# Reads ahead of rank passes, a table step inside the first product, and a reordered head and tail in a graph kernel

## The chip, the cores and the metric

The kernel runs on one core of a Trainium2 chip. The metric is the time of one execution on the device in microseconds (us); several runs are made and their median is taken. A profile of one further execution gives every instruction's start and duration, and the TensorE clock that was granted.

## The reference

x holds 32 graphs of 512 channels by 1024 nodes, f32. Layer 0 is an attention whose score for a pair of nodes is a leaky relu of a sum of two numbers, one of each node; layer 1 multiplies by the elementwise square of the adjacency, with its mask. Each layer is followed by a residual addition and a layer norm over the nodes.

```python
def _L0_gnn_ref(x, wq, wk, wm, bm):
    q = jnp.einsum('c,bcn->bn', wq, x)
    k = jnp.einsum('c,bcn->bn', wk, x)
    scores = q[:, None, :] + k[:, :, None]
    scores = jnp.where(scores > 0, scores, NEG_SLOPE * scores)
    att = jax.nn.softmax(scores, axis=-1)
    agg = jnp.einsum('bcn,bmn->bcm', x, att)
    out = jnp.einsum('oc,bcm->bom', wm, agg) + bm[None, :, None]
    return jax.nn.relu(out)

def _L1_gnn_ref(x, support, kernel, bias):
...
    W = support * kernel
    out = jnp.einsum('bnf,nm->bmf', x, W)
    out = out + bias
    return out

x = _layernorm(x + _L0_gnn_ref(x, L0_gnn_wq, L0_gnn_wk, adj, L0_gnn_bm), axis=-1)
x = _layernorm(x + _L1_gnn_ref(x, adj, adj, L1_gnn_bias), axis=-1)
```

## The kernel before

**Layer 0 without the matrix of scores.** A score depends on the sum of q of one node and k of another, so each side of the leaky relu is a product of an exponential of q and one of k. The nodes are sorted by q. Then, for every node, the nodes with a positive score are one end of the sorted list and the rest the other, and a softmax-weighted sum is a combination of two prefix sums, looked up at the place where k cuts the list. The steps for one graph:

- `project`: for each of 8 groups of 128 nodes, TensorE multiplies x by the weights with wq and wk beside them (8 matmuls of 128x257 into a PSUM tile `zp`); ScalarE copies it to `zrow`. Column 0 is q, the last column k.
- `peak`: VectorE takes the maximum of q and sets k aside. `spread` spreads q over the partitions (TensorE transposes `qb`, `mx`).
- `place`: the rank passes. For each of 8 node groups VectorE compares 128x1024 numbers and sums up (`lt`, 1.28 us), and a small instruction makes the index `ranki` of each pair of groups. `send` (GpSimd) writes the rows of `zrow` to DRAM (`td`) in sorted order with an indirect DMA. `count` (ScalarE) finds where k cuts the list. `fetch` (SyncE's DMA queue) brings the sorted rows back in 9 blocks, `zs`.
- `weigh`: ScalarE makes the exponentials `w`, VectorE the triangular matrices `lq`; part 0 for the first table step, part 1 for the others. `table`: 9 steps (0 to 8) of running sums. Each has 8 matmuls into `tp`, a ScalarE copy to `ts`, one row of which GpSimd (L425) and one ScalarE copy into the blocks of the next step; SyncE stores `ts` to `td`. So each step waits for the row copies of the one before.
- `share` makes the indices, `pick` (GpSimd) gathers the rows with 8 indirect DMAs into `rows`. `own`, `norm`, `scale` and `gain` weigh and add the parts of a row (`shares` is `own` and `norm`). `turn` transposes and adds the bias with a relu, `join` adds the residual x and takes layer-norm statistics; `root`, `shift` and `apply` finish the norm, `y`.

**Layer 1** is a product with the 512x512 matrix w1 (adj squared elementwise, plus identity), written as 7 products of quarters, as in Strassen's method: A11, S1, S2, S3, A22, S4, A12. Each has two halves, `mul[2n]` and `mul[2n+1]` (m = 0, 1) of two accumulation steps. Their operands are `sums` T1 to T4 of quarters of y, which VectorE makes, and their results are combined by VectorE `reads`: c1 reads A11, c5 S1, u2 S2, u3 S3, "21" A22, "12" S4, "11" A12, while u4 and "22" only add what was read before.

**Tiles.** PSUM has three large tiles in the pool `ps_mm` and one in `ps_t`. A new tile waits until one is released by its last reader. So A22 needs the tile that c5 reads, S4 the one of u2.

**Order.** All is issued in an order written out by hand, and each engine (TensorE, VectorE, ScalarE, GpSimd, and the DMA queues of SyncE and ScalarE) works its own instructions off in that order. Three graphs are in work at a time. `begin` projects graphs 0 to 2 and sorts and tabulates graph 0; `opening` finishes graph 0 up to its norm. `slot(s)`, 29 times, projects graph s + 2 (`new`), tabulates s + 1 (`mid`), finishes layer 0 of s and normalises and stores s − 1 (`old`). It ends with `phase`: the product of s, with picks of `mid` and rank passes and sends of `new` in between. `end` finishes the last two graphs with `rest` (a product with a hook `after(i)` behind each half) and `last`.

In `phase` the order for VectorE is: ranks 0 and 1, T2, c1 first half, ranks 2 and 3, T3, c1 second half, T4, ranks 4 and 5, c5, ranks 6 and 7, u2, u3, u4, 22, 21, then `shares` of picks 0 to 3, 12, two gains, 11, two gains. For GpSimd it is picks 0, 1, sends 0, 1, picks 2, 3, sends 2, 3, pick 4, pick 5, sends 4, 5, pick 6, sends 6, 7, pick 7. The ninth table step of `mid` stands ahead of `phase`, behind `spread`.

In the preamble, ScalarE's queue loads wq, wk, bm (as 4-byte pieces, one for each partition) and the bias of layer 1; SyncE's queue loads adj, then x. VectorE has copies of the transposed weights (L196), wq and wk (L197, L198), the squaring (L202) and a subtraction of the bias (L209) in this order of the program; the page's lines below show when each ran. In the middle of `begin`'s third loop all 8 picks of graph 0 are issued, and a copy of one element (L807) stands ahead of `fetch(1)`: it reads a picked row and writes into `zs`, so that the larger part of the fetch starts behind the fourth pick.

Of the kernel before, what the change touches and what calls it, by code (L numbers as in the profile page):

```python
# [23 lines left out]
def gat_gcn_resnorm_kernel(  # L24
# [46 lines left out]
    nc = tc.nc  # L71
# [36 lines left out]
    wq_sb = const.tile([P, CT], F32, name="wq_sb")  # L108
    nc.scalar.dma_start(out=wq_sb, in_=wq.rearrange("(t p) -> p t", p=P))
    wk_sb = const.tile([P, CT], F32, name="wk_sb")  # L110
    nc.scalar.dma_start(out=wk_sb, in_=wk.rearrange("(t p) -> p t", p=P))
    bm_sb = const.tile([P, CT], F32, name="bm_sb")
    nc.scalar.dma_start(out=bm_sb, in_=bm.rearrange("(t p) -> p t", p=P))
    bias_bc = const.tile([P, N], F32, name="bias_bc")
    nc.scalar.dma_start(out=bias_bc, in_=bias.partition_broadcast(P))
# [50 lines left out]
    for b in range(3):  # L166
        for ct in range(CT):
            load(b, ct)

# [17 lines left out]
    for ct in range(CT):  # L187
        pt = ps_mm.tile([P, C], F32, name=f"pt_{ct}", tag="mm")
        for ot in range(CT):
            nc.tensor.transpose(  # L190
                pt[:, ot * P : (ot + 1) * P], adj_sb[:, ot, ct * P : (ct + 1) * P], ident
            )
        if ct % 2:
            nc.scalar.copy(wmT[:, ct, 1 : C + 1], pt)
        else:
            nc.vector.tensor_copy(wmT[:, ct, 1 : C + 1], pt)  # L196
    nc.vector.tensor_copy(wmT[:, :, 0], wq_sb)  # L197
    nc.vector.tensor_copy(wmT[:, :, C + 1], wk_sb)  # L198


    w1 = adj_sb
    nc.vector.tensor_tensor(w1, adj_sb, adj_sb, ALU.mult)  # L202
    for ct in range(CT):
        nc.vector.tensor_tensor(
            w1[:, ct, ct * P : (ct + 1) * P], w1[:, ct, ct * P : (ct + 1) * P], ident, ALU.add
        )
    lo, hi = slice(0, H), slice(H, N)

    nc.vector.tensor_tensor(bias_bc[:, hi], bias_bc[:, hi], bias_bc[:, lo], ALU.subtract)  # L209
# [4 lines left out]
    nc.vector.tensor_tensor(ws[:, 0], a21, a22, ALU.add)  # L214
    nc.vector.tensor_tensor(ws[:, 1], ws[:, 0], a11, ALU.subtract)
    nc.vector.tensor_tensor(ws[:, 2], a12, ws[:, 1], ALU.subtract)
    nc.vector.tensor_tensor(a21, a11, a21, ALU.subtract)
# [334 lines left out]
    def sums(b, *some):  # L552

        yt = ys[b]
        for name, a in some:
# [8 lines left out]
            nc.vector.tensor_tensor(t, of, less, ALU.subtract)  # L564

    def layer1(b):
# [10 lines left out]
        def make(w, y, m):  # L577
            if m == 0 or b == B - 1 and w in ("S4", "A12"):
                ops[b, w] = ps_mm.tile([P, 2, H], F32, name=f"o{w}_{b}_{m}", tag="mm")
            for a in range(CT // 2):  # L580
# [5 lines left out]
        def read(mt, half, w, m, *of):  # L586
# [5 lines left out]
            nc.vector.tensor_tensor(vs[b, mt][:, half], x0, x1, ALU.add)  # L592

        mul, get = [], {}
        for w, y in (
# [3 lines left out]
            for m in range(2):  # L599
                mul.append(lambda w=w, y=y, m=m: make(w, y, m))  # L600
# [41 lines left out]
    def rest(b, after):  # L642
# [3 lines left out]
        for i in range(len(mul)):  # L646
            mul[i]()
            if i == 0:
                sums(b, ("T2", 0), ("T2", 1), ("T3", 0), ("T3", 1), ("T4", 0), ("T4", 1))
# [7 lines left out]
    def last(b):  # L657
# [23 lines left out]
        def after(i):  # L681
# [5 lines left out]
            if i == 9:  # L687
                stats1(b, 2, 3)
                roots(b, 2, 3)
            if i == 10:  # L690
                half(0, 1)
            if i == 11:
                half(1, 1)
                ready(b, 2, 3)
            if i in (12, 13):
                whole(i - 12)

# [4 lines left out]
    def phase(s, mid, new):  # L702
# [8 lines left out]
        mul[0]()  # L711
# [15 lines left out]
        pick(mid, 4)  # L727
# [5 lines left out]
        pick(mid, 5)  # L733
# [3 lines left out]
        reads("c5")  # L737
        mul[6]()
        mul[7]()
        pick(mid, 6)  # L740
# [3 lines left out]
        reads("u2")  # L744
        mul[8]()
        mul[9]()
        pick(mid, 7)
# [14 lines left out]
    def begin():  # L762


        for z in range(NT):
            project(0, z, 0)
            project(0, z, 1)
        peak(0)
# [20 lines left out]
        for z in range(NT):  # L789
# [13 lines left out]
            if z == NT // 2 - 1:  # L803
                for mt in range(NT):
                    pick(0, mt)

                nc.vector.tensor_copy(zs[32:33, 0, 0:1], rows[32:33, NT // 2 - 1, 0:1])  # L807
# [4 lines left out]
            if z == NT - 2:  # L812
# [191 lines left out]
```

## Time and profile before

| | us |
|---|---|
| median of 3 runs | 2364.88 |
| lowest and highest | 2363.13, 2366.72 |
| the profiled execution | 2366.34 |
| its span, first to last instruction | 2364.3 |
| TensorE busy | 2192.9 (93%) |
| VectorE busy | 1998.5 (85%) |
| ScalarE busy | 1405.0 (59%) |
| GpSimd busy | 993.4 (42%) |
| mean granted clock | 0.979 |

The costliest groups of instructions:

| line, engine, tile | count | busy us | mean ns |
|---|---|---|---|
| L257 TensorE zp | 4096 | 941.2 | 382 |
| L491 VectorE rows (gain) | 512 | 372.9 | 750 |
| L416 TensorE tp (table) | 2304 | 323.1 | 400 |
| L316 VectorE lt (place) | 240 | 307.0 | 1279 |
| L437 GpSimd rows (pick) | 256 | 289.9 | 1133 |
| L326 GpSimd td (send) | 256 | 280.5 | 1096 |
| L425 GpSimd zs (row copy) | 256 | 175.5 | 686 |

PE is TensorE, DVE VectorE, ACT ScalarE, POOL GpSimd and SP SyncE; "SPq" and the like are the sequencers that issue. In a chain of waits each line has a start, a duration and what ran or was waited for. In a timeline a line has a start, a duration, the engine, the line of the kernel, the operation, the tiles (out <- in), their shapes and a count, and in brackets how long the engine had been idle before and what it waited for. A busy share of 93% does not say that TensorE sets the end: matmuls that wait in a short gap, and those at a lower clock, count as they ran.

### The profile page before, as it was taken

Reading aid. Unit: us, or ns where it says so; the run is one execution under the profiler, and the core shown is the slowest. Engines: PE = TensorE matmul, PEld = TensorE weight load, DVE = VectorE, ACT = ScalarE, POOL = GpSimd, SP = SyncE. Lnnn points to the kernel's source line nnn. Section 1 sums busy time; section 2 is a strip of 40 time slices with the busy share of each in tenths; the row PEclk is TensorE's granted clock in tenths of the full one; section 3 lists DMA queues with packets and bytes.
Section 4 is the critical chain, followed back from the end, with each engine's and each line's share of the span. In section 5 each row is a group of like instructions: output and inputs, shape, how many; then the busy total and the mean of one; then the engine's idle time right before and its main releaser. Section 6 shows DMA issues by size and latency. Waiting matters only on the chain.

```text
span 2364.3 us, 30993 instructions
## 1 busy us (share of the span) xinstructions
PE 2192.9 (93%) x9520; PEld 1382.7 (58%) x9520; DVE 1998.5 (85%) x4157; ACT 1405.0 (59%) x2185; POOL 993.4 (42%) x1291
## 2 busy tenths in 40 slices
PE   7859999999999999999999999999999999999765
PEld 6636555666655566655556665556665555666322
DVE  4259888888988988988888898898898888889877
ACT  1555566665556675556666555667555666655543
POOL 1324445434444533444543444453344454344331
PEclk9979999999999999999999999999999999999887
DMA  6567787777777777878777777776787877777641
GB/s 227 156 186 245 230 276 250 226 225 239 251 249 258 243 218 228 259 234 277 250 219 227 240 252 251 259 241 216 235 256 236 274 251 220 231 238 247 221 172 72
DMA packets 176982, 548.68 MB, mean 232 GB/s; under 512 B 26320, under 2 KB 26320, under 8 KB 176816
## 3 DMA queue, kind: packets, MB, share of 16 engines
q1 hardware_dynamic: 117744, 276.65, 39.5%
q0 software_dynamic: 57344, 269.52, 32.5%
q8 instruction: 76, 1.25, 0.2%
q14 instruction: 90, 0.74, 0.1%
q10 hardware_dynamic: 1728, 0.53, 0.1%
HBM read 338.17 MB, written 208.43 MB: 231 GB/s over the span
## 4 chain that ended last, share of the span: by engine, by line
DVE 43%; PE 37%; ACT 7%; issue 6%; DMA 4%; POOL 2%; SPq 0%; ACTq 0%; POOLq 0%; DVEq 0%
PE zp L257 23%; DVE lt L316 13%; DVE st L500 8%; PE oS L581 5%; DVE rows L564 5%; DVE v L592 4%; PE oA L581 4%; DVE y L538 4%; PE tp L416 3%; PE op L529 2%; DMA rows<-td,idx 2%; DVE v L523 2%; ACT y L521 2%; ACT y L533 1%; DVE mv L502 1%
## 5 line engine op out<-in xcount | busy, mean ns | idle before, releaser
L257 PE MATMUL zp<-wmT,x 128*128 128x257 f32 x4096 | 941.2, 382 | 0.0
L257 PEld LDWEIGHTS zp<-wmT,x 128*128 128x128 f32 x4096 | 759.7, 190 | 152.2 <-issue 43.7
L425 POOL COPY zs<-ts 1x513 f32<-1x513 f32 x256 | 175.5, 686 | 830.5 <-ACT ts L421 830.1
L491 DVE SCALAR_TENSOR_TENSOR rows<-rows,ra 128x512 f32<-128x512 f32 x512 | 372.9, 750 | 35.9 <-ACT rows L483 26.8
L416 PE MATMUL tp<-zs,lq 128*64 128x257 f32 x2304 | 323.1, 400 | 74.2 <-POOL zs L425 41.7
L437 POOL DMA_INDIRECT rows<-td,idx x256 | 289.9, 1133 | 202.6 <-issue 104.4
L326 POOL DMA_INDIRECT td<-zrow,ranki x256 | 280.5, 1096 | 126.3 <-DVE ranki L321 52.3
L316 DVE SCALAR_TENSOR_TENSOR lt<-qb,zrow,first 128x1024 int8<-128x1024 f32 x240 | 307.0, 1279 | 4.3
L421 ACT COPY ts<-tp 128x514 f32<-128x514 f32 x288 | 169.0, 587 | 188.9 <-PE tp L416 177.2
L459 ACT ACTIVATE ac<-s 128x4 f32<-128x4 f32 x64 | 13.3, 208 | 450.2 <-DVE s L458 450.2
L341 ACT ACTIVATE sg<-lq,kc 128x1024 int8<-128x1024 f32 x240 | 275.2, 1147 | 6.8
L416 PEld LDWEIGHTS tp<-zs,lq 128*64 128x64 f32 x2304 | 145.1, 138 | 214.9 <-POOL zs L425 67.0
L581 PE MATMUL oA<-y,adj_sb 128*128 128x512 f32 x512 | 236.7, 604 | 7.8 <-ACT y L521 4.7
L265 ACT COPY zrow<-zp 128x514 f32<-128x514 f32 x256 | 148.6, 581 | 142.1 <-PE zp L257 128.4
L581 PE MATMUL oS<-rows,ws 128*128 128x512 f32 x512 | 225.5, 592 | 0.0
L483 ACT ACTIVATE rows<-rows,ra 128x512 f32<-128x512 f32 x256 | 167.1, 713 | 55.7 <-DVE ra L470 55.7
L509 POOL TENSOR_TENSOR rs<-rs,mhalf 128x1 f32<-128x1 f32 x256 | 171.7, 671 | 21.3
L521 ACT ACTIVATE y<-y,nb,rs 128x1024 f32<-128x1024 f32 x128 | 158.4, 1237 | 34.1 <-DVE nb L515 33.3
L581 PEld LDWEIGHTS oA<-y,adj_sb 128*128 128x128 f32 x512 | 95.1, 191 | 129.4 <-issue 111.5
L538 DVE TENSOR_TENSOR y<-y,x 128x1024 f32<-128x1024 f32 x128 | 155.9, 1218 | 16.6 <-ACT y L533 16.5
L581 PEld LDWEIGHTS oS<-rows,ws 128*128 128x128 f32 x512 | 96.6, 189 | 123.1 <-issue 122.2
L500 DVE BATCH_NORM_STATS2 st<-y 128x6 f32<-128x512 f32 x256 | 164.2, 683 | 2.6
(103 smaller groups left out, 2587.4 us busy)
## 6 DMA issues: line engine op xcount, KB each, us to landing
x<-in_x_dram SPq DMA_DIRECT2D x128, 512.0 KB, 5.0
out_dram<-v SPq DMA_DIRECT2D x126, 512.0 KB, 2.7
td<-ts SPq DMA_DIRECT2D x512, 120.5 KB, 2.6
zs<-td SPq DMA_DIRECT2D x64, 602.3 KB, 7.1
zs<-td SPq DMA_DIRECT2D x64, 240.9 KB, 3.3
zs<-td SPq DMA_DIRECT2D x96, 120.5 KB, 3.6
td<-ts SPq DMA_DIRECT2D x64, 96.4 KB, 2.0
td<-zs SPq DMA_DIRECT2D x8, 514.0 KB, 8.9
```

Source lines behind the costliest of these rows:

```text
L257: nc.tensor.matmul(zp[:, h, 0:CE], xb[ct][:, nt * P : (nt + 1) * P], wmT[:, ct, h * CE : (h + 1) * CE], start=(ct == 0), stop=(ct == CT - 1),)
L316: nc.vector.scalar_tensor_tensor(lt, qs, zrow[:, nt, 0:1], first[:, o : o + N], ALU.subtract, ALU.is_lt, accum_out=rank[:, nt : nt + 1],)
L326: sc = nc.gpsimd.indirect_dma_start(out=td[:, :], out_offset=bass.IndirectOffsetOnAxis(ap=ranki[:, nt : nt + 1], axis=0), in_=zrow[:, nt, ...
L341: nc.scalar.activation(sg, qs, AF.Sign, bias=kc[:, nt : nt + 1], accum_out=sgn[:, nt : nt + 1])
L416: nc.tensor.matmul(tp[i * G : (i + 1) * G, h, 0:CE], lw[:, ks[i], :], zs[:, j, h * CE : (h + 1) * CE], start=True, stop=True,)
L425: by.tensor_copy(zs[0:1, to, 1:ZW], ts[0:1, 1:ZW])
L437: nc.gpsimd.indirect_dma_start(out=rows[:, mt, :], out_offset=None, in_=tds[b].rearrange("(s u) c -> s (u c)", u=3), in_offset=bass.Indire ...
L491: nc.vector.scalar_tensor_tensor(u, g[:, k, i, 1 : C + 1], ra[:, k, i : i + 1], u, ALU.mult, ALU.add)
L500: nc.vector.bn_stats(st[:, h, :], t[:, h * H : (h + 1) * H])
L521: nc.scalar.activation(t, t, AF.Identity, bias=nb, scale=rs)
L538: nc.vector.tensor_tensor(t, t, xs[b][ot], ALU.add)
L581: nc.tensor.matmul(ops[b, w][:, m, :], quarters[w][:, a, m * P : (m + 1) * P], part(y, a), start=(a == 0), stop=(a == CT // 2 - 1),)
```

## The change

The preamble loads wq, wk and bm as rows of 512 bytes into one tile `vec` and turns them with one transpose. The bias goes to SyncE's queue, behind the four loads of graph 0. The transposes and copies of the weights become `turn_weights`, called first in `begin`; the squaring, the quarters' sums and the subtraction of the bias become `square_weights`, called behind the projections of graph 0.

```diff
-    wq_sb = const.tile([P, CT], F32, name="wq_sb")
-    nc.scalar.dma_start(out=wq_sb, in_=wq.rearrange("(t p) -> p t", p=P))
...
+    vec = const.tile([3 * CT, P], F32, name="vec")
+    for i, a in enumerate((wq, wk, bm)):
+        nc.scalar.dma_start(
+            out=vec[i * CT : (i + 1) * CT, :], in_=a.rearrange("(t p) -> t p", p=P)
+        )
...
-    nc.scalar.dma_start(out=bias_bc, in_=bias.partition_broadcast(P))
...
             load(b, ct)
+        if b == 0:
+            nc.sync.dma_start(out=bias_bc, in_=bias.partition_broadcast(P))
...
+    def turn_weights():
+        pt = ps_t.tile([P, N], F32, name="pt_v", tag="t")
+        nc.tensor.transpose(pt[:, 0 : 3 * CT], vec, ident[0 : 3 * CT, 0 : 3 * CT])
+        nc.vector.tensor_copy(wmT[:, :, 0], pt[:, 0:CT])
+        nc.vector.tensor_copy(wmT[:, :, C + 1], pt[:, CT : 2 * CT])
+        nc.vector.tensor_copy(bm_sb, pt[:, 2 * CT : 3 * CT])
...
     def begin():
+        turn_weights()
         for z in range(NT):
             project(0, z, 0)
             project(0, z, 1)
+        square_weights()
         peak(0)
```

In `begin` only picks 0 to 3 of graph 0 are issued, and the copy L807 is gone. Picks 4 to 7, the first shares, scales and gains go to `opening`, behind the first table step of graph 1:

```diff
             if z == NT // 2 - 1:
-                for mt in range(NT):
+                for mt in range(NT // 2):
                     pick(0, mt)
-                nc.vector.tensor_copy(zs[32:33, 0, 0:1], rows[32:33, NT // 2 - 1, 0:1])
                 fetch(1)
...
-            if z == NT - 2:
-                shares(0, 0, NT // 2)
-                scale(0, range(NT // 2))
-        gain(0, range(NT // 2))
+    def opening():
+
         weigh(1, 0)
-    def opening():
         table(1, 0)
+        for mt in range(NT // 2, NT):
+            pick(0, mt)
+        shares(0, 0, NT // 2)
+        scale(0, range(NT // 2))
+        table(1, 1)
+        gain(0, (0, 1))
+        weigh(1, 1)
+        gain(0, (2, 3))
         peak(2)
-        table(1, 1)
-        weigh(1, 1)
+        table(1, 2)
         shares(0, NT // 2, NT)
+        table(1, 3)
         scale(0, range(NT // 2, NT))
-        gain(0, (4, 5))
-        table(1, 2)
-        gain(0, (6, 7))
-        table(1, 3)
+        gain(0, range(NT // 2, NT))
```

In `phase`, half A11,0 is split after its first accumulation step, and the ninth table step, the last shift and apply of y, and the applies of `old` stand between the two steps. c5 is read ahead of ranks 4 and 5, u2 ahead of ranks 6 and 7. In the last phase (`new` is 31) picks 4 to 7 stand behind the last send:

```diff
-        mul[0]()
+        mul[0]((0,))
+        table(mid, NB - 1, pool=ps_mm)
+        shift(0, s, CT - 1)
+        apply(0, s, CT - 1)
+        for mt in (2, 3):
+            if old is not None:
+                apply(1, old, mt)
+                store(old, mt)
+        mul[0]((1,))
         mul[1]()
...
-        pick(mid, 4)
+        if new < B - 1:
+            pick(mid, 4)
...
-        pick(mid, 5)
+        if new < B - 1:
+            pick(mid, 5)
+        reads("c5")
         rank(4, 5)
         send(new, 4)
         send(new, 5)
-        reads("c5")
...
+        reads("u2")
         rank(6, 7)
         send(new, 6)
         send(new, 7)
-        reads("u2")
         mul[8]()
         mul[9]()
-        pick(mid, 7)
+        for mt in (7,) if new < B - 1 else (4, 5, 6, 7):
+            pick(mid, mt)
         fetch(new)
```

`make` takes the accumulation steps that it is to issue (`some`). In `end` and `last`:

```diff
             mul[i]()
             if i == 0:
+                after(-1)
+                shift(0, b, CT - 1)
+                apply(0, b, CT - 1)
                 sums(b, ("T2", 0), ("T2", 1), ("T3", 0), ("T3", 1), ("T4", 0), ("T4", 1))
...
-            if i in (0, 2, 4):
-                table(mid, CT + 2 + i // 2)
+            if i in (-1, 2, 4):
+                table(mid, CT + 2 + (i + 1) // 2)
...
-        for k in (0, NT // 2):
-            shares(mid, k, k + NT // 2)
-            scale(mid, range(k, k + NT // 2))
-            gain(mid, range(k, k + NT // 2))
+        shares(mid, 0, 2)
+        scale(mid, (0, 1))
+        own(mid, 2, 4)
+        gain(mid, (0,))
+        norm(mid, 2, 4)
+        scale(mid, (2, 3))
+        gain(mid, range(1, 4))
+        shares(mid, 4, NT)
+        scale(mid, range(4, NT))
+        gain(mid, range(4, NT))
...
-            nc.vector.tensor_tensor(t, of, less, ALU.subtract)
+            by = nc.gpsimd if b == B - 1 and name in ("T3", "T4") else nc.vector
+            by.tensor_tensor(t, of, less, ALU.subtract)
...
-            nc.vector.tensor_tensor(vs[b, mt][:, half], x0, x1, ALU.add)
+            by = nc.gpsimd if b == B - 1 and not w else nc.vector
+            by.tensor_tensor(vs[b, mt][:, half], x0, x1, ALU.add)
...
-            if i == 9:
+            if i in (10, 11):
+                half(i - 10, 1)
+            if i == 11:
                 stats1(b, 2, 3)
                 roots(b, 2, 3)
-            if i == 10:
-                half(0, 1)
-            if i == 11:
-                half(1, 1)
-                ready(b, 2, 3)
             if i in (12, 13):
                 whole(i - 12)
+            if i == 12:
+                ready(b, 2, 3)
```

So the differences T3 and T4 and the additions u4 and 22 of the last graph run on GpSimd; the statistics of its rows 2 and 3 are taken two halves of a product later than before, and their shift, apply and store stand behind the half A12,0.

## The prediction

> **What bounds it now.** The page's share of the chain of waits comes first: no engine bounds the whole.
>
> ```profile
> DVE 43%; PE 37%; ACT 7%; issue 6%; DMA 4%; POOL 2%; SPq 0%; ACTq 0%; POOLq 0%; DVEq 0%
> ```
>
> VectorE and TensorE hand the end to each other. So I read the stages one by one: the chain of one slot (peak at 799.26 us; all slots have the same pattern), the timeline around the places where it changes engine, then the first 200 us and the last 140. The timeline of the slot, with its waits in brackets:
>
> ```profile
> 800.43 1.09 PE L416 MATMUL tp<-zs,lq 128*64 128x257 f32 x8 [0.58 <-POOL zs L425]
> 816.57 3.70 PE L581 MATMUL oA<-rows,adj_sb 128*128 128x512 f32 x8 [1.11 <-DVE v L592]
> 820.52 3.70 PE L581 MATMUL oS<-y,ws 128*128 128x512 f32 x8 [0.26 <-DVE v L592]
> ```
>
> TensorE waits three times in a product, 0.58 for a table's row copy and 1.11 and 0.26 until VectorE has read a PSUM tile (c5, u2). It ends late, and the next stage shows who pays:
>
> ```profile
> 757.69 15.81 PE L257 MATMUL zp<-wmT,x 128*128 128x257 f32 x72
> 773.10 0.48 DVE L396 TENSOR_TENSOR lq<-tri,w 128x128 f32<-128x128 f32 x2
> 773.43 1.28 PE L416 MATMUL tp<-zs,lq 128*64 128x257 f32 x8
> ```
>
> 72 projections follow the product without a gap; the first table step behind them needs lq too, and starts 0.34 us behind the start of lq where that is late (137.33 after 136.99 in the opening). Measured from each slot's peak, in 27 of 28 slots the table starts at 43.98 because TensorE is not free sooner, while lq starts at 42.97 in the mean (42.41 to 44.43). lq0 lies 6.77 behind the second "own", which starts at 35.65 at the earliest (VectorE is busy without a gap from 2.9 on) or 0.12 after the last pick has landed (35.0 to 37.5).
>
> The head and the tail, chain and timeline:
>
> ```profile
> 2.48 12.72 DMA bias_bc<-in_L_gnn_bias_dram
> ...
> 17.69 28.72 PE zp L257 x128
> ```
> ```profile
> 15.22 0.69 DVE L209 TENSOR_TENSOR bias_bc<-bias_bc 128x512 f32<-128x512 f32 x1 [3.37 <-DMA bias_bc<-in_L_gnn_bias_dram]
> 15.83 1.28 DVE L196 COPY wmT<-pt 128x512 f32<-128x512 f32 x2
> ...
> 123.83 0.14 DVE L807 COPY zs<-rows 1x1 f32<-1x1 f32 x1 [28.72 <-DMA rows<-td,idx]
> 124.00 2.74 SPq L374 DMA_DIRECT2D zs<-td  x6
> ...
> 137.33 2.25 PE L416 MATMUL tp<-zs,lq 128*64 128x257 f32 x8 [15.57 <-DVE lq L396]
> ```
> ```profile
> 2222.28 7.68 DMA rows<-td,idx
> ...
> 2283.27 10.80 DMA rows<-td,idx
> ```
>
> The first projections wait for a bias that they don't need, because a VectorE subtraction of it stands ahead of the weight copies. In the opening the one-element copy L807 holds the fetch until four picks have landed, and TensorE idles 15.57 us. At the end two waits for gathered rows lie on the path.
>
> **The preamble.** The vectors become rows of 512 bytes and are turned by one transpose; the bias goes to SP behind four loads of x; its subtraction and the squaring go behind 64 tiles of projection. adj landed at 7.11, the last memset ends at 9.0. Three small copies (0.1 to 0.17 each by L197, L198), the first big copy 0.7, then the fourth group of transposes at about 10.4 instead of 16.57 and the projection at about 11.5 instead of 17.48: −6.0. The bound: x0's later tiles land at 11.48 and after, so −5 to −6.5. What moves behind costs VectorE 2.29 (L202) and some 4.4 in smaller pieces, under 28.7 us of projection; without that cover it would be 6.7. SP gets one more issue of 0.5 us ahead of x1, which is needed 28 us later.
>
> **The opening.** Without the copy, fetch is issued when the ranks have landed, at about 104.7 (110.67 less 6.0), next to four picks instead of eight. Four picks of 0.79 MB and a fetch of 1.05 at the 420 GB/s that the trace shows at 120 us are 10 us: landed by 116 to 120, about where the projections end (121.77 − 6.0 = 115.8). Table(1,0) starts near 117.3 against 137.33. Picks 4 to 7 go out behind its row copy, at 120 to 125, and the last lands near 132.6 by the spacing (1.9) and the latency (5.4 to 8) of the eight before. own, norm and scale (1.7 + 0.75), eight gains (5.9): done at 141; before, 154.55. The first relu starts at 141.5 instead of 155.73: **−14**, the 6 of the preamble in it. Bounds −11 (picks one transfer and a half later) to −17 (two less); if only the preamble counted, −6.
>
> **Each phase.** Eight matmuls (0.43 each) are split by the table: four, table, four. The table now finds its row copy ready, so the 0.58 vanishes; it starts 0.35 later, which the picks behind it have as slack (the first pick starts anywhere from 6.9 to 8.05 and the last always at 28.7). c5 is read ahead of ranks 4 and 5, ending at 14.45 instead of 17.26, u2 ahead of 6 and 7, at 18.45 instead of 21.21. TensorE: A11 and S1 to 8.6, S2 to 12.0, S3 from 12.1 (second c1 read), A22 15.55, S4 19.0, A12 22.45, projections 26.05 instead of 28.24. What is delayed: ranki(4,5) and (6,7), by 1.2 at most on VectorE; their sends start at 21.1 and later than 25, the indices are there at 17.1 and 21.3, so GpSimd doesn't see it. VectorE does the same work in the same time; own and lq stay. So 72 projections end at 41.8, 2.2 earlier, but the table waits for lq + 0.34: the gain of a slot is 43.98 − (lq + 0.34), mean 0.705, 1.22 at the floor of 42.42, nothing at 43.64 and later. Over 28 slots 19.7; less 0.1 per slot for a later lq, and with one phase more: **−17**. Bounds 0 and −35.
>
> TensorE's many short waits become one of some 1.5 us ahead of the table. What a gap does to the granted clock, three rows of the timeline bound:
>
> ```profile
> 2255.39 1.09 PE L416 MATMUL tp<-zs,lq 128*64 128x257 f32 x8 [1.90 <-POOL zs L425]
> 166.16 1.98 PE L416 MATMUL tp<-zs,lq 128*64 128x257 f32 x8 [1.90 <-POOL zs L425]
> 2236.25 2.17 PE L416 MATMUL tp<-zs,lq 128*64 128x257 f32 x8 [13.00 <-DVE lq L396]
> ```
>
> After 1.90 idle the step ran once at full speed and once not, but the slow one stands in a stretch with many gaps. The slot is busy all round, so I take nothing and keep 0.89 per slot for a rival. The Trainium skill (TensorE: Matmul & The Clock Gate, "What's actually happening") puts the drop to half clock at an idle window of about 3.4 us; by it alone the gap would cost nothing. The row at 166.16 shows slow steps behind a shorter gap.
>
> **The last phase.** Picks 4 to 7 of the graph before the last go behind the last four sends. GpSimd does the same 16 issues, so the last pick goes out about 0.5 later (send 6 waits for its index), but the fetch can start some 4 us earlier (it started at 2228.16, when the last send had landed) and shares the DMA with those four: 1.05 MB at 420 GB/s are 2.5. The last pick landed at 2229.96, and from there own, scale, gain and lq lead straight to the table at 2236.25. 0.5 + 2.5 = **+3**; bounds +0.5 and +5 (a pick behind two transfers more). No cover: TensorE idles 13.00 there.
>
> **end().** The table steps come earlier, but the picks wait for other work on GpSimd (a root at 2278.27): 0. The two pairs taken first would have been ready sooner, but own(2,4) waits for the fourth pick (2294.06) as before; only six instructions of "norm" and a scale come out of the chain: −0.85. The moved shift and apply keep their time.
>
> **last().** GpSimd takes four differences (VectorE 0.61 each, −2.4 there) and u4, 22 (four of 0.61). Its two-input addition of 128x512 is not in the trace. Nearest rows: its 1x513 copy, 0.60 alone, is the low end; three times that, 1.8, the high end, since its sends and copies grow when VectorE adds two SBUF tiles (send 1.01 to 1.42 at 821.73). I take 1.2, two passes. The reads of A22 then wait for four of these, 4.8 against VectorE's other work of that stretch, and start 0.8 earlier; with the other delays **−0.4**. At 1.0: −1.2; at 1.8: +2.4.
>
> The Trainium skill speaks against such a move: GPSIMD Engine Reference, section 3.1, has a two-input addition of 2048 f32 at 4497 ns against 2293 on VectorE, by a quarter an estimate of 1.1 us for 512, at which the sum would be −0.8 here.
>
> **Sum** against the profiled execution, 2366.34 (span 2364.3 and 2.0 around it): −14 − 17 + 3 − 0.85 − 0.4 = −29.25, 2337.1. The median of the runs is 1.46 below that execution: **2336**.
>
> **The likeliest case,** 0.57: 2326 to 2348 by the bounds of opening, last phase and end.
>
> **Rival 1, lq at its floor,** 0.13: TensorE's earlier end relieves what makes picks late, and each of 29 phases gives 1.22, −35: 2318. For it: half of the slots lie within 0.45 of the floor. Against: picks land late because of GpSimd's and the DMA's own queue, which isn't shortened.
>
> **Rival 2, the clock,** 0.20: the gap ahead of the table costs 0.89 (1.98 − 1.09) to 1.08 (2.17 − 1.09) in each slot, more than 0.705 gives. 29 x 0.185 = +5: 2358; at 1.08, +11, 2364, no change. For it the row at 166.16; against it that at 2255.39.
>
> **Rival 3, slower: PSUM tiles by strict turn,** 0.10. The table's tile now comes after A11's in order. If tiles go round strictly, S2 gets A11's, which is held until the second c1 read at 12.1, not 8.6. Five halves of 3.43 behind that put the projections at 29.3, 1.1 later than now, in 30 phases +33: 2366.3 − 14 + 33 + 1.75 − 1.5 = 2386. It decides as soon as S2 starts behind c1. Against it: the placement of before gives three projection tiles in a row the banks 4, 0 and 4, so the tile that was released first is taken.
>
> **Chances.** A measurement of this kernel tells 0.2% (4.7 us) from no change. Faster: 0.57 + 0.13 + 0.15 of rival 2 = 0.85; same: 0.04 of rival 2; slower: 0.10 and 0.01 of rival 2. The range 2317 to 2358 takes in rival 1 and the milder half of rival 2.
>
> **What would show it.** Right: the first projection near 11.5, table(1,0) near 117, S2 behind S1 without a gap, projections 26.0 after the peak, the first table 0.34 behind lq at 43.3, slots of about 69.0. Wrong: lq later than 43.6, tables of 2 us in the slots, S2 starting at 12.1, a last phase whose final pick lands 35.1 after the peak, as now, GpSimd additions near 2 us.

## The result and the profile after

The changed kernel takes 2345.07 us (median of 4 runs, 2339.51 to 2346.60) against 2365.07 before (4 runs): a ratio of 0.9911, with a 95% interval of 0.9894 to 0.9929. It is 20 us faster; forecast were 29. Measured once more in another comparison (e12 below) it took 2341.74 against 2362.83, 0.9904 [0.9887, 0.9920]. The profiled execution has a span of 2342.9 us, 21.4 less than before.

Splitting both spans at the same events shows where the time came from. The columns of this table are differences of starts and ends in the two traces; "first table" is the first table step of graph 31, "last gain" the end of the last gain.

| stretch | before | after | difference | forecast |
|---|---|---|---|---|
| start to the first slot's peak | 239.42 | 228.53 | −10.9 | −14 |
| 28 slots, first peak to last | 1955.43 | 1942.22 | −13.2 | −17 |
| last peak to the first table | 41.39 | 45.71 | +4.3 | +3 |
| first table to the last gain | 74.45 | 72.40 | −2.05 | −0.85 |
| last gain to the end | 53.63 | 54.05 | +0.4 | −0.4 |

Each column is one execution, and all but the last row scatter. In the changed kernel and four later runs with the same opening (e4, e5, e11, e12) the first stretch took 227.4 to 232.3, mean 229.2; in e1 and e2, with the opening of before, it took 236.6 and 239.0. The second row and the last phase are treated under e12. The last row repeats within 0.04.

The page's share of the chain of waits of the changed kernel:

```profile
DVE 55%; DMA 13%; issue 10%; PE 9%; ACT 7%; POOL 5%; SPq 0%; ACTq 0%; DVEq 0%; POOLq 0%
```

TensorE had 37% of the chain and now has 9%: VectorE, and DMAs that VectorE waits for, set the end. The timeline of one slot shows it (peak at 782.80; the same products as those shown before, with the line numbers of the changed kernel):

```profile
784.18 1.09 PE L426 MATMUL tp<-zs,lq 128*64 128x257 f32 x8
785.20 2.84 PE L592 MATMUL oA<-y,adj_sb 128*128 128x512 f32 x6
787.88 7.03 PE L592 MATMUL oS<-rows,ws 128*128 128x512 f32 x16
...
798.49 3.60 PE L592 MATMUL oA<-rows,adj_sb 128*128 128x512 f32 x8
801.92 3.60 PE L592 MATMUL oS<-y,ws 128*128 128x512 f32 x8
...
808.80 15.92 PE L267 MATMUL zp<-wmT,x 128*128 128x257 f32 x72
825.73 0.65 PE L426 MATMUL tp<-zs,lq 128*64 128x257 f32 x3 [1.02 <-DVE lq L406]
```

None of the three waits of before is left, the projections start 26.00 after the peak (28.24 before), and one wait for lq stands in their place. That is the forecast picture: 26.0, and the table 0.34 behind lq (825.39).

The clock over the 28 slots, before and then changed: each row has the window, its length, the busy time of TensorE, of its weight loads, of VectorE, ScalarE and GpSimd, and then the granted clock, the DMA share and GB/s.

```profile
239.42:2194.85 1955.43, 1896.39 (x8319) 1196.38 (x8317) 1735.37 (x3612) 1221.80 (x1905) 865.23 (x1120) 1.00 0.76 242
```
```profile
228.53:2170.75 1942.22, 1898.73 (x8319) 1196.64 (x8318) 1734.60 (x3612) 1218.98 (x1905) 863.52 (x1120) 1.00 0.76 244
```

The granted clock is 1.00 in both; what brings the mean down to 0.979 and 0.977 lies in the head and the tail. The head and the opening, timeline:

```profile
10.76 1.47 PE L267 MATMUL zp<-wmT,x 128*128 128x257 f32 x6
...
118.39 1.36 PE L426 MATMUL tp<-zs,lq 128*64 128x257 f32 x8 [2.55 <-DVE lq L406]
...
123.48 0.17 DVE L466 TENSOR_TENSOR s<-rows,kc 128x4 f32<-128x4 f32 x1 [4.86 <-DMA rows<-td,idx]
...
135.91 0.17 DVE L466 TENSOR_TENSOR s<-rows,kc 128x4 f32<-128x4 f32 x1 [1.83 <-DMA rows<-td,idx]
```

The projections start 6.7 earlier, and the first table of graph 1 at 118.39 (137.33 before; forecast near 117). But both "own" of graph 0 now wait for gathered rows: the first four land at 123.4, the last four at 135.8. The last two waits of the end, again on picks, from the chain of the changed kernel:

```profile
2199.35 11.33 DMA rows<-td,idx
...
2267.52 12.90 DMA rows<-td,idx
```

### The profile page after: what moved, and what is told of

Same layout as the page of the kernel before. It is cut to its first block, busy times and chain, and to the rows that moved or that the text cites. A ratio compares the mean times of both kernels' runs of the same rounds, so it can differ in the third digit from the quotient of the medians.

```text
span 2342.9 us, 30955 instructions
## 1 busy us (share of the span) xinstructions
PE 2200.9 (94%) x9521; PEld 1385.4 (59%) x9521; DVE 1995.4 (85%) x4156; ACT 1402.6 (60%) x2186; POOL 1001.9 (43%) x1299
## 3 DMA queue, kind: packets, MB, share of 16 engines
q8 instruction: 76, 1.25, 0.2%
## 4 chain that ended last, share of the span: by engine, by line
DVE 55%; DMA 13%; issue 10%; PE 9%; ACT 7%; POOL 5%; SPq 0%; ACTq 0%; DVEq 0%; POOLq 0%
DVE lt L326 13%; DMA rows<-td,idx 10%; DVE v L604 9%; DVE st L510 8%; DVE rows L501 6%; PE zp L267 5%; DVE rows L575 5%; DVE y L548 4%; PE tp L426 3%; POOL td L336 3%; DVE v L533 2%; PE op L539 2%; ACT y L531 2%; ACT y L543 1%; DVE lq L406 1%
## 5 line engine op out<-in xcount | busy, mean ns | idle before, releaser
L426 PE MATMUL tp<-zs,lq 128*64 128x257 f32 x2304 | 328.4, 400 | 83.8 <-DVE lq L406 66.2
L469 ACT ACTIVATE ac<-s 128x4 f32<-128x4 f32 (+1 forms) x65 | 13.6, 209 | 501.5 <-DVE s L468 413.6
L426 PEld LDWEIGHTS tp<-zs,lq 128*64 128x64 f32 x2304 | 150.1, 139 | 243.3 <-DVE lq L406 72.6
L592 PE MATMUL oA<-y,adj_sb 128*128 128x512 f32 x512 | 245.1, 612 | 7.0 <-ACT y L531 4.7
L539 PE MATMUL op<-ident,rows 128*128 128x128 f32 x1024 | 148.2, 288 | 26.6 <-DVE rows L501 26.6
```

The costliest lines, as they stand in the source:

```text
L426: nc.tensor.matmul(tp[i * G : (i + 1) * G, h, 0:CE], lw[:, ks[i], :], zs[:, j, h * CE : (h + 1) * CE], start=True, stop=True,)
L592: nc.tensor.matmul(ops[b, w][:, m, :], quarters[w][:, a, m * P : (m + 1) * P], part(y, a), start=(a == 0), stop=(a == CT // 2 - 1),)
```

## The experiments

Unless a comparison over several runs is named, each is one profiled execution. Its stretches are then read from the trace, since single times scatter by several us.

### e1: the reads alone

The kernel before, with two moves:

```diff
+        reads("c5")
         rank(4, 5)
...
-        reads("c5")
+        reads("u2")
         rank(6, 7)
...
-        reads("u2")
```

> The kernel before, with only c5 read ahead of ranks 4 and 5 and u2 ahead of 6 and 7. Theory (the early reads carry the steady gain): the projections start 26.3 us after the peak (before 28.2, changed kernel 26.0), the table then waits for lq and takes 1.28 us; a slot falls from 69.84 to 69.3-69.4 in the mean, the span by 13 (to 2351). Rival (reads and table share the gain): projections near 27, half of the gain, span 2357 to 2358.

Span 2344.8. Timeline of the slot with its peak at 788.86:

```profile
790.03 1.09 PE L416 MATMUL tp<-zs,lq 128*64 128x257 f32 x8 [0.58 <-POOL zs L425]
...
804.89 3.60 PE L581 MATMUL oA<-rows,adj_sb 128*128 128x512 f32 x8
808.33 3.60 PE L581 MATMUL oS<-y,ws 128*128 128x512 f32 x8
...
815.19 15.81 PE L257 MATMUL zp<-wmT,x 128*128 128x257 f32 x72
831.64 1.28 PE L416 MATMUL tp<-zs,lq 128*64 128x257 f32 x8 [0.63 <-DVE lq L396]
```

A22 and S4 no longer wait; the projections start 26.33 after the peak with the 0.58 still there, and then the table waits for lq. The 28 slots take 1939.7, 15.7 less than before, 69.28 in the mean, within what the slots of the changed kernel take in six traces (1932 to 1942, under e12). So the two reads carry the steady gain, as far as these runs can tell.

### e2: the table inside the product alone

```diff
-        mul[0]()
+        mul[0]((0,))
+        table(mid, NB - 1, pool=ps_mm)
...
+        mul[0]((1,))
         mul[1]()
```

> The kernel before, with only the table step (and the applies) inside the first product. Theory: nothing is gained by itself, since A22 still waits until c5 has been read at 17.3 after the peak; projections at 28.2, slots 69.8, span within 1.5 of 2364.3. Rival (the 0.58 that TensorE waited ahead of the table comes out of each slot): projections at 27.6, slots 69.3, span 2350.

Span 2361.8. Timeline, peak at 797.03:

```profile
814.34 3.70 PE L581 MATMUL oA<-rows,adj_sb 128*128 128x512 f32 x8 [1.46 <-DVE v L592]
818.30 3.70 PE L581 MATMUL oS<-y,ws 128*128 128x512 f32 x8 [0.26 <-DVE v L592]
...
825.27 15.81 PE L257 MATMUL zp<-wmT,x 128*128 128x257 f32 x72
```

The projections start at 28.24, as before. What was saved ahead of the table is waited for at A22 (1.46 for 1.11), since c5 is read when it was. The 28 slots take 1952.9, 2.6 less than before, in slots whose TensorE rows look the same: no more than the scatter of this stretch, shown below. Beside the reads the inside table brings the start of the projections from 26.33 to 26.00, ahead of a wait for lq, where nothing is seen of it.

### e3: the loads, transposes and squaring alone

The preamble and the first lines of `begin` from the changed kernel, the rest as before.

> The kernel before, with only the loads, the transposes and the squaring of the changed kernel. Theory: first projection at 10.9 instead of 17.5 and the first peak at 39.4 instead of 47.1; the shift of 7.6 goes on unchanged through the opening, so the first slot's peak comes at 231.8 (before 239.4, changed kernel 228.5) and the span is 2356.7. Rival (the opening waits for DMA in any case and takes part of it back): peak at 234 or later, span over 2358.

First projection 10.88, first peak 40.47 (6.6 earlier than before), the first slot's peak 234.14 (5.3 earlier), span 2358.5. The numbers are those of the rival, but one execution doesn't decide between 231.8 and 234: one and the same opening ends between 227.4 and 232.3, and e1, with the head of before, has its peak at 236.6 where before has 239.4. So some 5 us of the first stretch belong to the head and some 5 to the changed opening, each to within 2 or 3.

### e4 and e11: the last phase's picks where they were

```diff
-        if new < B - 1:
-            pick(mid, 4)
+        pick(mid, 4)
...
-        for mt in (7,) if new < B - 1 else (4, 5, 6, 7):
-            pick(mid, mt)
+        pick(mid, 7)
```

> The changed kernel, with the last phase's picks 4 to 7 where they were. Theory (they delay own, and own delays lq): from the last peak to the table 41.4 instead of 45.7, so 4.3 less; the rest of the end unchanged, span 2338.6. Rival (the earlier fetch pays later, or own's wait only moves to the weights): table at 43 or later, span 2341 or more.

Span 2334.9. The table comes 41.36 after the last peak, as it was foretold; the last gain follows it by 74.00 instead of 72.40, so of the 4.35 only 2.75 reach the end in this pair. That is scatter: behind the table, the four other traces with the picks at the end (e12 and e5 to e7) take 73.2 to 74.3. The rest of the difference of 8.0 lies in the slots (1937.3 against 1942.2), where nothing differs. So it was timed:

> The changed kernel with the last phase's picks where they were, timed. Theory: 2.75 less than the changed kernel from the last peak on, with nothing else different: ratio to the kernel before 0.9890 to 0.9905 (changed kernel 0.9911), 2338 to 2343 us. Rival (the single run of 2336.8 was the picks' luck in the slots and nothing is gained): 2345.

2334.33 against 2364.56, a ratio of 0.9876 [0.9862, 0.9890]: the fastest version of this study. The gain is larger than the 2.75; to see how much of it was chance, the changed kernel was measured again.

### e12: the changed kernel again

> The changed kernel itself once more. Theory (the last phase's picks cost it 2.75 and the rest of the distance to the version with them back, 10.7 between the medians, is the scatter of when the last pick of each slot lands): ratio to the kernel before 0.988 to 0.990, 2336 to 2341 us. Rival (the picks' place costs the whole 10.7): 2344 or more again, ratio 0.991 or more.

2341.74 against 2362.83, 0.9904. Between the two forecasts: the 10.7 between the medians was partly scatter, but the place of the picks is worth more than 2.75. The "own" behind the last pick, timelines of the changed kernel, of e12 and of e11 (one line each):

```profile
2210.80 0.16 DVE L466 TENSOR_TENSOR s<-rows,kc 128x4 f32<-128x4 f32 x1 [4.35 <-DMA rows<-td,idx]
```
```profile
2205.87 0.16 DVE L466 TENSOR_TENSOR s<-rows,kc 128x4 f32<-128x4 f32 x1 [6.57 <-DMA rows<-td,idx]
```
```profile
2195.32 0.16 DVE L466 TENSOR_TENSOR s<-rows,kc 128x4 f32<-128x4 f32 x1 [0.23 <-DMA rows<-td,idx]
```

VectorE waits 4.35, 6.57 and 0.23 for the last pick. From the last peak to the last gain, the five traces with the picks at the end (the changed kernel, e12, e5, e6, e7) have 118.1, 122.1, 121.2, 120.6, 121.2, mean 120.63; the five with the same end and the picks in place (e4, e11 and e8 to e10) 114.6 to 115.7, mean 115.16. The picks' move costs **5.5**, and the first profile of the changed kernel had the mildest case.

The 28 slots of the six traces whose slots and phases issue the same (the changed kernel, e4, e5, e6, e11, e12) take 1942.2, 1937.3, 1935.2, 1936.4, 1932.1 and 1934.1, mean 1936.2; the three with the slots of before or equal to them in time (before, e2, e3) 1955.4, 1952.9 and 1954.5, mean 1954.3. The slots' gain is 18 by the means, 13 by the first profile.

### e5: the last sums on VectorE

```diff
-            by = nc.gpsimd if b == B - 1 and name in ("T3", "T4") else nc.vector
-            by.tensor_tensor(t, of, less, ALU.subtract)
+            nc.vector.tensor_tensor(t, of, less, ALU.subtract)
...
-            by = nc.gpsimd if b == B - 1 and not w else nc.vector
-            by.tensor_tensor(vs[b, mt][:, half], x0, x1, ALU.add)
+            nc.vector.tensor_tensor(vs[b, mt][:, half], x0, x1, ALU.add)
```

> The changed kernel, with the last graph's T3, T4, u4 and 22 on VectorE again. Theory (GpSimd's additions of 1.24 us make VectorE wait 2.9 at the A22 reads and hold two small VectorE instructions for about 2, against 4.9 of work saved): from the last gain's end to the end of the span 54.0 plus or minus 0.4, as with GpSimd (54.05) and as before (53.6). Rival (the offload saves at least the 2.4 of the four differences): 56 or more.

53.87 from the last gain to the end, against 54.05: as the theory has it, GpSimd's help is worth nothing. It even costs some 0.2: this stretch takes 54.02 to 54.06 in all nine traces with GpSimd's sums, and 53.62 or 53.63 in the four with the end of before. The other 0.2 of the +0.4 are thus not GpSimd's; what remains changed behind the last gain is the place of the statistics, shifts and applies, which no run has put back. The timeline of the changed kernel shows what eats up the help (GpSimd's additions, then what VectorE does beside them):

```profile
2318.98 2.50 POOL L604 TENSOR_TENSOR v<-v,v 128x512 f32<-128x512 f32 x2
2321.44 2.49 POOL L604 TENSOR_TENSOR v<-v 128x512 f32<-128x512 f32 x2
```
```profile
2305.42 1.21 DVE L525 SCALAR_TENSOR_TENSOR nb<-mv,rs 128x1 f32<-128x1 f32 x1 [1.07 <-POOL rs L519]
...
2319.05 1.28 DVE L525 SCALAR_TENSOR_TENSOR nb<-mv,rs 128x1 f32<-128x1 f32 x2
2322.74 0.69 DVE L604 TENSOR_TENSOR v<-oA,v 128x512 f32<-128x512 f32 x1 [2.41 <-POOL v L604]
2323.96 0.69 DVE L604 TENSOR_TENSOR v<-oA,v 128x512 f32<-128x512 f32 x1 [0.53 <-POOL v L604]
```

An addition takes 1.25 on GpSimd, twice VectorE's 0.61 or so. The A22 reads overwrite what "22" still reads, so they wait 2.41 and 0.53 for it. And an instruction of one number for each partition, "nb", which takes 0.11 to 0.16 in this stretch where GpSimd stands idle, takes 1.21, and two of them 1.28, beside a GpSimd addition. Every slot has the same on a smaller scale: one nb takes 0.56 or 0.57, and ends together with one of GpSimd's row copies (at 780.45 beside the copy from 780.00 to 781.00).

The Trainium skill (SBUF — State Buffer, "SBUF: two separate sides") calls the ports that VectorE and GpSimd share an exclusive lock, held for a whole instruction; the nb lines agree, in a case with all operands in SBUF on both engines.

### e6: all eight picks of graph 0 at once

```diff
                 fetch(1)
+                for mt in range(NT // 2, NT):
+                    pick(0, mt)
...
         table(1, 0)
-        for mt in range(NT // 2, NT):
-            pick(0, mt)
         shares(0, 0, NT // 2)
```

> The changed kernel, with picks 4 to 7 of graph 0 issued right behind picks 0 to 3 and fetch, not behind the first table step of graph 1. Theory (GpSimd stands idle from 110 to 120 and the last picks land at 135.8 only because they are issued at 121 to 125): last pick lands by 127, the last gain ends at 138 to 140 instead of 144.6, the first slot's peak at 222 to 225 (228.3 now). Rival (the fetch then shares the DMA with eight picks, and the table starts late): table at 121 or later instead of 118.4, peak at 227 or later.

The rival, though by another piece than it named: the first table starts at 119.35, but the second part of the exponentials waits for the rest of the fetch. Timelines of VectorE in e6 and in the changed kernel, the second lq of graph 1:

```profile
134.85 1.03 DVE L406 TENSOR_TENSOR lq<-tri,w 128x384 f32<-128x384 f32 x2 [5.64 <-ACT w L398]
```
```profile
129.31 1.03 DVE L406 TENSOR_TENSOR lq<-tri,w 128x384 f32<-128x384 f32 x2 [0.39 <-ACT w L398]
```

The peak of the first slot comes at 233.3, but e5, with the opening of the changed kernel, has it at 232.3. Clear of the scatter is the stretch from the first table to the first relu: 30.8 here, 26.9 to 27.9 in nine traces with the picks in two halves. And the last gather lands at 136.18 though it was issued at 114.71; in the changed kernel it was issued at 125.18 and landed at 135.8. Eight gathers beside the fetch push the fetch's end, and the gathers are bound by the DMA more than by when GpSimd issues them.

### e7 to e10: the wait for lq

After the change each slot waits for lq. Four versions tried to take this wait away. e7 moves the exponentials of the first table step one project earlier:

```diff
             if z == 1:
+                weigh(mid, 0)
                 scale(s, (6, 7))
                 gain(s, (6,))
             if z == 2:
-                weigh(mid, 0)
                 gain(s, (7,))
```

> The changed kernel, with the exponentials and lq of the first table step one project earlier in each slot, ahead of scales 6 and 7 and gain 6. Theory (the slot now waits for lq, and the 1.28 us of the first table step come from the second lq instruction, not from the clock): table 42.0 after the peak instead of 43.4, its eight matmuls 1.09 us; VectorE's 0.57 idle ahead of the second lq part goes, slots 68.8 in the mean, the stretch from the first to the last slot's peak 1937 to 1942 less 16, so 1921 to 1926. Rival 1 (VectorE sets the slot anyway, lq only trades places with a gain): slots unchanged. Rival 2 (the clock): the step takes 1.28 also when it doesn't wait.

The table starts at 42.11 in the mean instead of 43.39, and where it doesn't wait its eight matmuls take 1.09. But the slot takes 69.43 (69.37 in the changed kernel's first profile, 69.0 to 69.4 in its six traces). Timeline of e7, TensorE at the end of the slot with its peak at 367.01:

```profile
408.86 1.09 PE L426 MATMUL tp<-zs,lq 128*64 128x257 f32 x8
409.88 0.98 PE L539 MATMUL op<-ident,rows 128*128 128x128 f32 x7
411.86 0.33 PE L539 MATMUL op<-ident,rows 128*128 128x128 f32 x1 [1.00 <-DVE rows L501]
```

The first rival is right, and the rows show the mechanism: the wait goes from lq to the transposes "op" right behind the table, which need the last gain (1.17 in the mean of the 28 slots). Both lie at the end of VectorE's work behind "own". The second rival falls, and with it, for the changed kernel, the prediction's own rival about the clock: there the step takes 1.28 only because its second group of matmuls waits for the second of the two lq instructions (lq at 825.39 and 825.59, the first matmul at 825.73, the second at 825.93).

e8 adds a move of one statistic (`stats1(old, 0)`) ahead of the second "own", to fill VectorE's wait for the last pick, with the picks of e4; e9 is the same without the earlier lq.

> The changed kernel with the last phase's picks where they were, the first lq one project earlier, and one of the two statistics of the old graph (two instructions and an aggregate, 1.45 us) moved from behind gain 7 to ahead of the second own. Theory (a slot is now VectorE's chain from own, which waits 0.48 in the mean for the last pick, over lq to the second lq part): own always at 37.1 after the peak without a wait, table at 42.9, second lq part at 47.8 to 47.9 instead of 48.4; slots 68.7 to 68.8 in the mean, the 28 slots together 1924 to 1927. Rival (what comes behind own only moves by what is put ahead of it): second lq part at 48.4 or later, 1937 or more.

> The same without the earlier lq. Theory: own at 37.1, lq 6.77 behind it at 43.9, table at 44.2 and, 5.0 behind the table, the second lq part at 49.2 instead of 48.4: slots 0.8 longer, near 70.1, the 28 slots 1960 to 1964. Rival (VectorE's total work sets the slot, in whatever order): 48.0 and 1925 to 1930 as with the earlier lq.

e8 missed: slots 70.12, 1963.3 for 28, the second lq part at 49.17. e9 came as expected: 70.16, 1964.5, 49.25. Whatever is put ahead of "own" delays what comes behind it: in e9 the table waits for lq, and in e8, with the earlier lq, the transposes wait for the last gain (1.14 in the mean), as in e7.

e10 takes the transposes out of the way, behind the second half of the project and the second exponentials (`turn(s, 0)` behind `weigh(mid, 1)`), with e7's order and e4's picks.

> The changed kernel with the last phase's picks where they were, the first lq one project earlier, and the first turn of each slot moved on TensorE from ahead of a project's second half to behind it and behind the second exponentials. Theory (with an early lq the wait only moves to that turn, which needs the last gain, 1.13 us in the runs with the early lq): projections go on behind the table without a wait, second lq part at 47.8 instead of 48.4, slots 68.7 to 68.8, the 28 slots 1924 to 1927; together with the picks 2322 to 2326 us. Rival (the slot's length is set by VectorE's work behind own, whatever TensorE does): slots 69.3 or more, time 2337 or more.

2367.75 against 2364.56, 1.0012 [1.0000, 1.0024]; 33 slower than e11. The second lq part came at 47.75 in the median, as expected, but the slots take 70.39. Timelines of e10, ScalarE and then TensorE, in the slot with its peak at 442.10:

```profile
489.69 0.69 ACT L398 ACTIVATE w<-zs,bw,el 128x7 f32<-128x7 f32 x2 [1.59 <-DMA zs<-td]
490.28 1.09 ACT L543 ACTIVATE y<-op,bm_sb 128x1024 f32<-128x1024 f32 x1
491.28 0.57 ACT L431 COPY ts<-tp 128x514 f32<-128x514 f32 x1
```
```profile
488.28 1.09 PE L426 MATMUL tp<-zs,lq 128*64 128x257 f32 x8
489.30 2.01 PE L267 MATMUL zp<-wmT,x 128*128 128x257 f32 x8
493.15 1.16 PE L426 MATMUL tp<-zs,lq 128*64 128x257 f32 x8 [1.85 <-POOL zs L435]
```

The second exponentials come so early that they wait for the rest of the fetch, and ScalarE with them; behind them stands the relu of the moved transposes, and only then the copy of the second table step (done on TensorE at 489.4), whose row the third step waits for, 1.85. The fetch of the sorted rows and ScalarE's order are thus further limits at the same place. The clock is one more. The gap ahead of the third step is 1.2 to 2.24 us, and in eight of the 28 slots the granted clock then falls to half for 3.4 us. The timeline of such a slot, and its windows (TensorE's busy time, clock, DMA share, GB/s):

```profile
563.80 2.05 PE L426 MATMUL tp<-zs,lq 128*64 128x257 f32 x8 [2.24 <-POOL zs L435]
```
```profile
560.40:563.80 3.40, 1.17 (x6) 1.00 0.25 71
563.80:567.20 3.40, 3.40 (x15) 0.51 0.21 81
```

These eight slots last 71.9 in the mean, the other twenty 69.8, still more than the 69.0 to 69.4 of the changed kernel. Neither the theory nor the rival had named these limits.

## Why the prediction was right, and where it was off

**The range and the sign held**: 2345 in 2317 to 2358 and within the likeliest case, whose mechanism came in each stretch but the last. The size was off by 9: 29 forecast, 20 measured (21 in e12). The slots gave what was forecast; the opening gave 4 to 5 less, the last phase cost some 2.5 more and the end 0.8 more. Over several traces two terms lie outside their own bounds (opening, last phase), and a range of 41 us was wide enough to take that in.

**Each phase: mechanism right, size within the scatter.** Forecast −17; −13.2 in the first profile, −18.1 by the means over traces. The start of the projections (26.0), the first table at lq + 0.34 and lq later by 0.08 (0.1 in the forecast) came as worked out. One term was missing: the first table step takes 1.28 when it waits for lq, 0.19 more than behind the projections, 5.3 in 28 slots. The prediction's own line at 773.43, one of two slots (it counts one) in which the table of before waited for lq, had it: lq consists of two instructions, and the step's matmuls need both. What paid it back was luck: the forecast was read from one trace with lq at 42.97 and had it 0.1 later, 43.07, while in the mean of six traces it came at 42.87 (e2 and e3, whose slots are as long as those of before, have 42.80 and 42.92). What the prediction credited to the two edits together belongs to the reads (e1, e2).

**The opening: −14 forecast, −10.9 in the first profile, 9 to 10 by the traces with either opening.** The preamble was right where it was priced: 6.7 at the first projection in this pair, 5.5 against e1 and e2, which start at 16.3 with the head of before; forecast 6.0. The step that failed is "the last lands near 132.6": the last pick landed at 135.8, 10.6 behind its issue at 125.18, where the forecast took about 7.5 from the eight before. The gains' end went to 144.6 instead of 141 and the first relu to 145.3 instead of 141.5. Two sizes behind that step were wrong. The first is the fetch. The page of before has these transfers for the 32 graphs:

```profile
zs<-td SPq DMA_DIRECT2D x64, 602.3 KB, 7.1
zs<-td SPq DMA_DIRECT2D x64, 240.9 KB, 3.3
zs<-td SPq DMA_DIRECT2D x96, 120.5 KB, 3.6
```

For one graph these are 2.1 MB; the prediction has 1.05, here and in the last phase. The second is the rate: from 112 to 132 the DMA engines are busy without a pause, but they move 248 to 419 GB/s, not 420 throughout (windows of the changed kernel: length, GpSimd's busy time, clock, DMA share, GB/s):

```profile
112.00:116.00 4.00, 0.00 (x0) 1.00 1.01 316
116.00:120.00 4.00, 0.00 (x0) 0.99 1.01 307
120.00:124.00 4.00, 2.72 (x4) 0.50 1.00 248
124.00:128.00 4.00, 1.87 (x2) 0.50 1.04 320
128.00:132.00 4.00, 1.11 (x1) 0.50 1.02 419
```

A part of the fetch landed at 123.7 in e4 and 127.6 in e5, where the forecast had all of it by 116 to 120. So the queues still had work when picks 4 to 7 came: the first of them landed 8.7 to 9.2 behind its issue in the five traces that tell single landings (e4, e5, e7 to e9), for the 5.4 to 8 of the forecast. (Of the eight picks of before only the first three took 5.4 to 8; the last, issued at 120.22, landed at 134.76.) That this is the reason is read from these numbers and from e6; no run has changed the fetch alone.

**The last phase: +3 forecast, +4.3 in the first profile, +5.7 by the mean of five.** The sign was right: this edit makes the kernel slower, and undoing it gives the fastest version. The sum was 0.5 for a later issue and 2.5 for the fetch. The last pick was issued 28.6 after the peak instead of 27.4, but that isn't the picks' doing: with the picks in place it is 28.57 in e4, and 28.64 in e2, so it comes with the table inside the product. What was mis-sized is the fetch's share of the DMA: the last pick landed 11.3 behind its issue (11.3 to 13.0 in the changed kernel and e5 to e7), against 7.7 before and 7.0 in e4. With 2.1 MB the prediction's own sum would have 5.0 for its 2.5, and +5.5 in all.

**end(): −0.85 forecast.** From the last peak to the last gain the five traces with the new end and the picks in place have 115.2 in the mean, the four with the old end (before, e1 to e3) 115.8: −0.6, within the scatter of either group (114.6 to 115.7 and 114.8 to 116.3). The −2.05 of the first profile is not its worth: the four other traces with the picks at the end take 73.2 to 74.3 from the table to the last gain, against 72.40 there.

**last(): −0.4 forecast, +0.4 measured.** GpSimd's addition was sized right (1.2 for 1.25; at 1.8 the working gives +2.0, not its +2.4), and the wait of the A22 reads was foreseen. What failed is "start 0.8 earlier": the first of these reads starts 33.9 behind the last gain instead of 34.3, and the second, which waits once more, 35.1 instead of 34.9. GpSimd also holds up VectorE's small instructions; the sum had this contention only in GpSimd's own time. Together that took what was saved (e5: 53.87 without, 54.05 with). The estimate of 1.1, worked out from the Trainium skill's figure for 2048 elements (GPSIMD Engine Reference, section 3.1), was near the 1.25.

**Rivals.** The strict turn of PSUM tiles didn't come: S2 follows S1 in one row of 16 matmuls (787.88); the bank numbers that the prediction gives against this rival stand in no trace, the row alone decides. The clock didn't come in the changed kernel: 1.00 over the slots, and no step of 2 us behind gaps of 0.8 to 1.6. It was a fair rival all the same: in e10, behind gaps of 1.8 to 2.24, it came in eight slots. lq at its floor didn't come: "own" waited for the last pick as before.

## What to carry to other kernels

When two engines hand the end to each other, the gain of freeing one is the slack of the other: measure that slack slot by slot, and look for the next two chains that end at the same place before moving anything more. A DMA issued later costs more than its delay if it then shares the queues with another; a work list moved to an idle engine is only worth it if no one waits for it and if it doesn't lock what the busy one needs. Where single profiles differ by more than the edit under test, read the stretch that the edit touches, and over several traces.

## What the runs showed of the hardware

A gap of 0.8 to 1.6 us ahead of a table step, in every slot, left the granted clock at 1.00 over the 28 slots and the step at 1.28 us. In e10, gaps of 1.2 to 2.24 us a little later in the slot were followed in eight of 28 slots by 3.4 us at half clock, with a step of 2.05. The table step behind 19.55 us of idle in the last phase (at 2216.46) took 2.19 by the chain. A GpSimd addition of 128x512 f32 takes 1.25 us, and a VectorE instruction of 0.16 that starts beside it takes 1.21. Eight gathers of 0.79 MB each beside a fetch of 2.1 MB (e6), instead of four, put the exponentials that need the whole fetch 15.1 us behind the first table step, waiting 5.29 for it; in the nine traces with four they start 10.5 to 12.1 behind it, without a wait. The landing of the last gather of a slot scatters between slots (VectorE's own starts 35.6 to 38.1 after the peak in one execution); the 28 slots of one and the same order took 1932 to 1942 us.
